# Two expert loops cut at 58 and 54 blocks with the rest in a branch, and a routing step moved ahead of an earlier branch

## The chip, the cores and the metric

The kernel runs on one core of a Trainium2 chip. The metric is device time in microseconds (us), the median of several runs. A core has five engines with instruction queues of their own: TensorE (PE) for matrix products, VectorE (DVE), ScalarE (ACT), GpSimd (POOL) and SyncE (SP). SP, ACT and POOL also issue DMA transfers. Engines wait for each other through semaphores. A branch in the program is taken by each engine for itself.

## What is computed

Two layers, each a graph network and then a mixture of experts, on x of 3125 nodes with 256 features and 50000 edges. Each of the four parts reads the layer-normalized x and is added to x. Only the mixtures matter here:

```python
# layer 0: 16 experts, the best 2 of a softmax, weighted
top_probs, top_idx = jax.lax.top_k(probs, 2)
dispatch = sum(one_hot(top_idx, 16) * (top_probs / sum(top_probs))[..., None], -2)
hidden = silu(x @ w1[e]) * (x @ w2[e])          # 512 wide, for each expert e
x = x + sum_e dispatch[:, e] * (hidden @ w3[e])
# layer 1: 8 experts, the best 2 of the scores, unweighted
h = gelu(x @ W1[e] + b1[e])                     # 512 wide
x = x + sum_e mask[:, e] * (h @ W2[e] + b2[e])
```

Every node picks two experts, so 6250 rows of work are shared out unevenly over the experts.

## The kernel before

The program runs in stages. Layer 0's graph part works on the transposed adjacency counts, in panels of 512 columns (convolution1, convolution2). While the last convolution's panels end, Router.panel finds for each node its two experts and its rank within each expert. A flag tells whether the edges came sorted; where they did not, a branch (L884 and L885) builds the graph in another way and repeats the layer. With these inputs the branch isn't taken, but each engine loads the flag, compares, and jumps over the code. At the place where it arrives it raises its own semaphore by the count of the code it left out; whoever comes after the branch waits for that arrival.

Behind the branch stand three steps. First, resident (L906): GpSimd issues 16 loads of 0.5 MB each, which bring w3 of all experts into SBUF (w3_all, 8.39 MB). Second, Router.route: rows of an expert are packed into blocks of 128 rows, no block mixes experts, and route works out for each block its expert (exp, expi) and its 128 node numbers (idx). It starts from the totals of each expert (L604, L607), forms each expert's first block (L622), compares block numbers with each node's block (L645, a vector operation of 64 x 25 elements a partition), multiplies by tile and row numbers (L649 on ScalarE, L650 on VectorE), and sums with 50 small matrix products (L652); three vector operations then make idx (L657 to L661). Third, experts.

How many blocks there are isn't known when the program is built. The kernel runs the largest number that can occur:

```python
def blocks_of(n_exp):
    return (2 * N + n_exp * (P - 1)) // P     # 64 for 16 experts, 56 for 8
```

Blocks beyond the last real one have a spare row as each of their nodes and cost the same work. In experts, a block does this: begin (SP loads the w1 and w2 of its expert, L934, into one of three buffers each; GpSimd gathers its 128 rows from DRAM with an indirect DMA, L940), hidden (TensorE transposes the rows, L401, and multiplies with the weights, L961: 8 products in layer 0, 4 in layer 1, where the weights all stay in SBUF), finish (TensorE transposes the hidden rows, L973, multiplies with w3, L980, VectorE makes y, L996 or L988, and GpSimd adds y to the rows in DRAM with an indirect DMA, L997). Blocks are begun two ahead, and finished two behind in layer 0, one behind in layer 1. GpSimd executes its queue in order: w3's 16 loads, then gathers and scatters as the blocks come. Its DMAs use eight completion semaphores in turn, so that a ninth waits for the first to land.

After layer 0's blocks, the next stage loads x from the same DRAM rows (xb0, L1045), and waits for all scatters. After layer 1's, one copy from DRAM to DRAM (L1215) brings the result out, which also waits for all scatters. The edges' flag decides a second branch, with an else, around layer 1's graph part (L1187).

Of the kernel before, what the change touches and what calls it, by code (L numbers as in the profile page):

```python
# [18 lines left out]
P = 128  # L19
# [33 lines left out]
def kernel(ctx: ExitStack, tc: tile.TileContext, a, out: bass.AP):  # L53
# [81 lines left out]
    def build_sorted(c):  # L135

        found = keep.tile([1, 1], F32, name="found")
        free = onehots[:, 3 * GW * (NF + P) :]  # L140
        sums = free[:, : 4 * NG].bitcast(F32)
        ohr = free[:, 4 * NG :][:, : P * WN].rearrange("p (w r) -> p w r", r=WN)
        gl = c.enter_context(tc.tile_pool(name="sl", bufs=1))
        gk = c.enter_context(tc.tile_pool(name="sk", bufs=2))

        def iota_of(pool, name, shape, pattern, base=0, mult=0, dtype=F32):
# [344 lines left out]
    def blocks_of(n_exp):  # L491
        return (2 * N + n_exp * (P - 1)) // P

    class Router:


# [2 lines left out]

        ohs_ = keep.tile([P, 2, NT, NE0], F16, name="ohs")  # L500
        high = keep.tile([P, 2, NT], F32, name="high")
        before_ = keep.tile([P, NT + 1, NE0], F16, name="before")

        def __init__(self, n_exp):
            self.n = n_exp
            self.ohs = self.ohs_[:, :, :, :n_exp]
            self.before = self.before_[:, :, :n_exp]
            self.rows = onehots.rearrange("p (c t r) -> p c t r", c=2, t=NT)

        def panel(self, small, c0, s, gates=None):  # L510
            n_exp, n, t0 = self.n, s.shape[1], c0 // P
# [80 lines left out]
                )  # L592

        def route(self, small):


            n_exp = self.n
            nb = blocks_of(n_exp)

            def tile_(name, shape, dtype=F32):  # L600
                return small.tile(shape, dtype, name=name)

            pc = ps_one("totals", [P, n_exp])
            nc.tensor.matmul(pc, ones16, self.before[:, NT, :], start=True, stop=True)  # L604

            cnt = tile_("cnt", [P, n_exp])
            nc.vector.tensor_scalar(cnt, pc, float(P - 1), None, op0=OP.add)  # L607
            cnti = tile_("cnti", [P, n_exp], I32)
            nc.vector.tensor_copy(cnti, cnt)
            nc.vector.tensor_single_scalar(cnti, cnti, 7, op=OP.arith_shift_right)  # L610
            nblk = tile_("nblk", [P, n_exp])
            nc.vector.tensor_copy(nblk, cnti)
            ends = [tile_(f"ends{i}", [P, n_exp]) for i in range(2)]
            nc.vector.tensor_copy(ends[0], nblk)
            d, cur = 1, 0
            while d < n_exp:
                nc.vector.tensor_add(ends[1 - cur][:, d:], ends[cur][:, d:], ends[cur][:, : n_exp - d])
                nc.vector.tensor_copy(ends[1 - cur][:, :d], ends[cur][:, :d])
                d, cur = 2 * d, 1 - cur
            ends = ends[cur]  # L620
            first = tile_("first", [P, n_exp], F16)
            nc.vector.tensor_sub(first, ends, nblk)  # L622

            past = tile_("past", [P, nb, n_exp])
            nc.vector.tensor_tensor(
                past, iota[:, :nb, None].to_broadcast([P, nb, n_exp]), ends[:, None, :].to_broadcast([P, nb, n_exp]),
                OP.is_ge,
            )
            exp = keep.tile([P, nb], F32, name=f"exp{n_exp}")
            nc.vector.tensor_reduce(exp, past, AX.X, OP.add)  # L630
            nc.vector.tensor_scalar(exp, exp, float(n_exp - 1), None, op0=OP.min)
            expi = keep.tile([1, nb], I32, name=f"expi{n_exp}")
            nc.vector.tensor_copy(expi, exp[:1])

            pi = ps_one("nodes", [P, 2, nb])
            for c in range(2):
                of = tile_("of", [P, NT, n_exp], F16)
                nc.vector.tensor_tensor(of, self.ohs[:, c], first[:, None, :].to_broadcast([P, NT, n_exp]), OP.mult)
                blk = tile_("blk", [P, NT])
                nc.vector.tensor_reduce(blk, of, AX.X, OP.add)  # L640
                blk16 = tile_(f"blk16_{c}", [P, NT], F16)
                nc.vector.tensor_add(blk16, blk, self.high[:, c, :])
                is_ = tile_(f"is_{c}", [P, nb, NT], F16)
                shape = [P, nb, NT]
                nc.vector.tensor_tensor(  # L645
                    is_, iota16[:, :nb, None].to_broadcast(shape), blk16[:, None, :].to_broadcast(shape), OP.is_equal
                )
                what = tile_(f"what{c}", [P, 2, nb, NT], F16)
                nc.scalar.activation(what[:, 1], is_, AF.Copy, scale=pcol)  # L649
                nc.vector.tensor_tensor(what[:, 0], is_, tiles16[:, None, :].to_broadcast(shape), OP.mult)  # L650
                for t in range(NT):
                    nc.tensor.matmul(  # L652
                        pi.rearrange("p a b -> p (a b)"), self.rows[:, c, t, :], what[:, :, :, t].rearrange("p a b -> p (a b)"),
                        start=(c == 0 and t == 0), stop=(c == 1 and t == NT - 1),
                    )
            none = tile_("none", [P, nb])
            nc.vector.tensor_scalar(none, pi[:, 0, :], 0.0, spare, op0=OP.is_equal, op1=OP.mult)  # L657
            node = tile_("node", [P, nb])
            nc.vector.scalar_tensor_tensor(node, pi[:, 0, :], float(P), none, op0=OP.mult, op1=OP.add)
            idx = keep.tile([P, nb], I32, name=f"idx{n_exp}")  # L660
            nc.vector.scalar_tensor_tensor(idx, node, -float(P), pi[:, 1, :], op0=OP.add, op1=OP.add)  # L661
            return idx, exp, expi


    class First:
# [147 lines left out]
    with ExitStack() as c:  # L813
# [62 lines left out]
        with ExitStack() as c1:  # L876
# [4 lines left out]
                nc.scalar.dma_start(t[NP:, :], behind[:, : t.shape[1]])  # L881
            f.weights2(c1)
            convolution2(f, False, c1.enter_context(tc.tile_pool(name="loads0", bufs=3)))
    sorted_ = nc.values_load(flag, min_val=0, max_val=1)  # L884
    with tc.If(sorted_ == 0):  # L885
        build_graph()
        degrees(0, NT)
        with ExitStack() as c:
# [7 lines left out]
            open_rows(c)  # L896
            f.weights2(c)
            convolution2(f, True, c.enter_context(tc.tile_pool(name="loads0", bufs=3)))


    def resident(pool, name, w):
# [4 lines left out]
            nc.gpsimd.dma_start(t[:, e], w[e].rearrange("(k p) n -> p k n", p=P))  # L906
        return t

    def experts(hids, wts, xnd, xb, n_exp, idx, expi, w_in, b_in, w_out, act, gated=None, b_out=None, stay=(), depth=1):

        n_in, n_hid = len(w_in), w_out.shape[1] // P
        stay = list(stay) + [None] * (n_in + 1 - len(stay))
        streamed = b_in is not None or None in stay
        wide = D if gated is None else D + 4

        sent, ran, regs = [], [], {}

# [32 lines left out]
            if any(t is not None for t in stay):  # L952
                regs[b] = expert_of(nc.tensor, ran, b)

        def hidden(b, weights, bi, xg):
            xT = hids.tile([P, KD, P], F32, name="xT")
            transpose_tile(xT, xg)
            ph = ps_wide("ph")
            for i in range(n_in):
                for k in range(KD):  # L960
                    ran.append(nc.tensor.matmul(  # L961
                        ph[:, i, :], xT[:, k, :], weight_of(b, weights, i, k), start=(k == 0), stop=(k == KD - 1)
                    ))
                    if i + k == 0 and b + 1 < nb:
                        register(b + 1)
            hid = hids.tile([P, n_hid * P], F32, name="hid", bufs=depth + 1)
            act(hid, ph, bi)
# [2 lines left out]
        def finish(b, hid, weights, xg):  # L970
# [13 lines left out]
                mine, bo = b_out  # L984
                nc.tensor.matmul(po, mine[:, b : b + 1].to_broadcast([mine.shape[0], P]), bo, start=False, stop=True)  # L985
            y = hids.tile([P, D], F32, name="y", bufs=2)
            if gated is None:
                nc.vector.tensor_copy(y, po)  # L988
            else:
                each = hids.tile([P, 2], F32, name="each")  # L990
                gate = hids.tile([P, 1], F32, name="gate")
                nc.vector.scalar_tensor_tensor(  # L992
                    each, xg[:, D + 2 :], gated[:, b : b + 1], xg[:, D : D + 2], op0=OP.is_equal, op1=OP.mult,
                    accum_out=gate,
                )
                nc.vector.tensor_scalar(y, po, gate, None, op0=OP.mult)  # L996
# [2 lines left out]
                in_=y, in_offset=None, compute_op=OP.add,  # L999
            )  # L1000

        nb = blocks_of(n_exp)
        register(0)
        ahead = [begin(0), begin(1)]
        open_ = []
        for b in range(nb):
            weights, bi, xg = ahead.pop(0)
            open_.append((b, hidden(b, weights, bi, xg), weights, xg))
            if len(open_) > depth:
                finish(*open_.pop(0))  # L1010
            if b + 2 < nb:
                ahead.append(begin(b + 2))
        for o in open_:
            finish(*o)

    ffn0 = ctx.enter_context(ExitStack())
    w3_all = resident(ffn0.enter_context(tc.tile_pool(name="res0", bufs=1)), "w3_all", a["L0_ffn_w3"])
    with ExitStack() as c:
        idx, exp, expi = router0.route(c.enter_context(tc.tile_pool(name="small0", bufs=1)))

    with ExitStack() as c:
        hids = c.enter_context(tc.tile_pool(name="hids0", bufs=2))
        wts = c.enter_context(tc.tile_pool(name="wts0", bufs=3))
# [1 line left out]
        def silu_gate(hid, ph, bi):  # L1025
# [1 line left out]
            nc.vector.tensor_mul(hid, hid, ph[:, 1, :])  # L1027

        experts(
            hids, wts, xnd0, xb0, NE0, idx, expi,  # L1030
            [a["L0_ffn_w1"], a["L0_ffn_w2"]], None, a["L0_ffn_w3"], silu_gate, gated=exp, stay=[None, None, w3_all], depth=2,
        )
    ffn0.close()

# [159 lines left out]


    with ExitStack() as c:
        idx, exp, expi = router1.route(c.enter_context(tc.tile_pool(name="small1", bufs=1)))
        mine = keep.tile([NE1, blocks_of(NE1)], F32, name="mine")
        nc.vector.tensor_scalar(mine, exp[:NE1], pcol[:NE1], None, op0=OP.is_equal)

    with ExitStack() as c:
        hids = c.enter_context(tc.tile_pool(name="hids1", bufs=2))
# [4 lines left out]
        def gelu(hid, ph, bi):  # L1207
# [1 line left out]
            nc.scalar.activation(hid, hid, AF.Gelu)  # L1209

        experts(
            hids, wts, xnd1, xb1, NE1, idx, expi, [a["L1_ffn_W1"]], a["L1_ffn_b1"], a["L1_ffn_W2"], gelu,
            None, (mine, b2e), [w1_all, w2_all],
        )
    nc.sync.dma_start(out, xb1[:N, :])  # L1215

# [30 lines left out]
```

## Time and profile before

| | |
|---|---|
| median of 3 runs | 1919.1 us (1915.95 to 1920.69) |
| the profiled execution, its span | 1919.9 us, 1918.1 us |
| busy: PE, DVE, ACT, POOL | 86%, 47%, 36%, 27% of the span |
| gathers and scatters of blocks | 120 each |
| blocks of layer 0 | about 671 to 1079 us |
| blocks of layer 1 | about 1596 to 1905 us |

A row of the timeline has the start in us from the span's start, the duration, the engine, the line, the operation, what it writes and reads, and how often; in brackets stands how long the engine was idle before it and what ended that. PE is busy nearly without a gap in both stretches of blocks. The stretch between 624 and 672 us, in which the choice of experts ends, is one of the idlest of the execution: PE is busy 16.2 of 48 us.

### The profile page before, as it was taken

The page shows a single profiled execution, that of the slowest core. Times are in us where ns is not written, and L with a number is a line of the kernel's source. Part 1 is how long each engine was busy: PE and PEld are TensorE (multiplying, and loading weights), DVE is VectorE, ACT ScalarE, POOL GpSimd, SP SyncE. Part 2 cuts the span into 40 slices and gives each one's busy share as a digit, 9 for nine tenths or more (in the row PEclk, how much of TensorE's full clock was granted, in tenths as well). Part 3 has the DMA queues.
Part 4 walks back from the last instruction along what each step waited for, and adds up shares of the span by engine and source line. Part 5 has one row for each costly group of instructions (what it writes and reads, how often), then busy time and mean ns, then how long its engine had stood idle before and what let it go on. Part 6 is the DMA issues. An engine that isn't in the chain of part 4 may idle for free. (4 is left out here: it accounts for less than half of the span.)

```text
span 1918.1 us, 24044 instructions
## 1 busy us (share of the span) xinstructions
PE 1652.2 (86%) x7618; PEld 1127.4 (59%) x7618; DVE 893.1 (47%) x2509; ACT 682.5 (36%) x1596; POOL 509.8 (27%) x543
## 2 busy tenths in 40 slices
PE   4899999799998399999999459789797647999995
PEld 3777777677777155665556336456565534556553
DVE  5866665246665423322233457456467452222221
ACT  2766666234442122222222246346363102222221
POOL 4411110100000334444443234014021202445442
PEclk9999999999998599999999769999998657999998
DMA  3311111611110687777777220000012603444444
GB/s 116 104 47 47 48 48 37 224 59 56 56 59 24 202 247 216 218 213 211 211 217 192 63 60 0 1 1 1 1 34 66 233 28 76 102 102 99 101 103 102
DMA packets 126765, 193.02 MB, mean 101 GB/s; under 512 B 15040, under 2 KB 71727, under 8 KB 126559
## 3 DMA queue, kind: packets, MB, share of 16 engines
q1 hardware_dynamic: 93036, 137.34, 22.6%
q0 software_dynamic: 28544, 50.74, 12.7%
q10 hardware_dynamic: 5042, 3.23, 0.6%
q8 instruction: 67, 1.10, 0.2%
q14 instruction: 76, 0.61, 0.1%
HBM read 148.74 MB, written 45.72 MB: 101 GB/s over the span
## 5 line engine op out<-in xcount | busy, mean ns | idle before, releaser
L723 PE MATMUL pa<-blk,hl 128*128 128x512 f32 (+1 forms) x1400 | 366.9, 401 | 1.3 <-ACT blk L434 1.3
L997 POOL DMA_INDIRECT xb<-y,idx x120 | 190.9, 1591 | 326.7 <-DVE each L992 221.2
L723 PEld LDWEIGHTS pa<-blk,hl 128*128 128x128 f32 x1400 | 249.3, 196 | 43.7 <-ACT blk L434 1.8
L434 ACT CAST blk<-at 128x512 fp32r<-128x512 fp8e4 (+1 forms) x378 | 208.3, 572 | 137.2 <-PE pa L723 59.4
L961 PE MATMUL ph<-w,xT 128*128 128x512 f32 x512 | 238.8, 610 | 5.6 <-ACT xT L402 0.8
L980 PE MATMUL pe<-w_all,hTs 128*128 x960 | 227.2, 379 | 3.0 <-ACT hTs L976 3.0
L980 PEld LDWEIGHTS pe<-w_all,hTs 128*128 128x128 f32 x960 | 182.1, 190 | 78.1 <-issue 55.5
L436 DVE CAST blk<-at 128x512 fp32r<-128x512 fp8e4 (+1 forms) x392 | 167.8, 438 | 93.2 <-PE pa L723 56.4
L1136 PE MATMUL pc<-blk,g 128*128 128x512 f32 (+1 forms) x525 | 150.2, 420 | 23.9 <-ACT blk L434 13.7
L940 POOL DMA_INDIRECT xg<-xnd,idx x120 | 117.9, 982 | 168.4 <-DVE idx L661 86.0
L961 PEld LDWEIGHTS ph<-w,xT 128*128 128x128 f32 x512 | 92.6, 191 | 114.4 <-issue 88.3
L402 ACT COPY xT<-pt 128x256 f32<-128x256 f32 x195 | 72.6, 372 | 227.8 <-PE pt L401 226.0
L1027 DVE TENSOR_TENSOR hid<-hid,ph 128x512 f32<-128x512 f32 x64 | 44.0, 688 | 232.8 <-ACT hid L1026 232.8
L438 POOL CAST blk<-at 128x512 fp32r<-128x512 fp8e4 (+1 forms) x105 | 66.1, 629 | 292.2 <-PE pc L1136 290.3
L1136 PEld LDWEIGHTS pc<-blk,g 128*128 128x128 f32 x525 | 92.7, 201 | 66.2 <-DVE blk L436 22.3
L1026 ACT ACTIVATE hid<-ph 128x512 f32<-128x512 f32 x64 | 38.2, 597 | 219.4 <-PE ph L961 219.4
L961 PE MATMUL ph<-w_all,xT 128*128 x224 | 112.0, 624 | 4.2
L271 ACT ACTIVATE at<-pcount 128x400 fp8e4<-128x400 f32 x196 | 97.4, 502 | 49.4 <-PE pcount L267 48.2
L267 PE MATMUL pcount<-onehots 128*128 128x100 f16 x784 | 93.8, 270 | 3.0 <-ACT at L271 1.5
L267 PEld LDWEIGHTS <-onehots 128*128 128x128 f16 x784 | 68.8, 118 | 28.3 <-issue 12.8
L906 POOL DMA_DIRECT2D w_all<-in_L_ffn_w_dram x16 | 12.1, 767 | 268.2 <-PE totals L604 263.6
L1209 ACT ACTIVATE hid<-hid 128x512 f32<-128x512 f32 x56 | 35.3, 630 | 133.8 <-DVE hid L1208 133.8
(250 smaller groups left out, 2284.2 us busy)
## 6 DMA issues: line engine op xcount, KB each, us to landing
w<-in_L_ffn_w_dram SPq DMA_DIRECT2D x128, 512.0 KB, 4.7
bin<-in_L_ffn_b_dram SPq DMA_DIRECT2D x56, 256.0 KB, 3.5
w_all<-in_L_ffn_w_dram POOLq DMA_DIRECT2D x16, 512.0 KB, 10.7
w_all<-in_L_ffn_W_dram POOLq DMA_DIRECT2D x16, 512.0 KB, 10.8
h1d<-hl SPq DMA_DIRECT2D x25, 256.0 KB, 2.0
hl<-h1d SPq DMA_DIRECT2D x25, 256.0 KB, 5.3
xp<-in_x_dram SPq DMA_DIRECT2D x12, 512.0 KB, 4.7
mine<-own SPq DMA_DIRECT2D x12, 512.0 KB, 3.9
```

The lines of the kernel that those rows point to most:

```text
L267: nc.tensor.matmul(pw[:, w * NF : (w + 1) * NF], ohl[:, b, :, w], ohk[:, b, :, w], start=True, stop=True)
L271: nc.scalar.activation(at8[o // PW][:, :, o % PW : o % PW + 4 * WN].rearrange("p k (w r) -> p w k r", r=WN), pw[:, : 4 * NF].rearrange("p ...
L402: nc.scalar.copy(dst, pt)
L434: nc.scalar.copy(dst, src)
L436: nc.vector.tensor_copy(dst, src)
L438: nc.gpsimd.tensor_copy(dst, src)
L723: nc.tensor.matmul(pa[:, m, :w], parts[k][:, i, m * P : (m + 1) * P].bitcast(one), blk, start=(k == 0 and i == 0), stop=(k == NT - 1 and i ...
L940: nc.gpsimd.indirect_dma_start(out=xg, out_offset=None, in_=xnd[:, :], in_offset=bass.IndirectOffsetOnAxis(ap=idx[:, b : b + 1], axis=0),)
L961: ran.append(nc.tensor.matmul(ph[:, i, :], xT[:, k, :], weight_of(b, weights, i, k), start=(k == 0), stop=(k == KD - 1)))
L980: nc.tensor.matmul(po, hT[:, j, :], weight_of(b, weights, n_in, j), start=(j == 0), stop=(j == n_hid - 1 and b_out is None))
L997: nc.gpsimd.indirect_dma_start(out=xb[:, :], out_offset=bass.IndirectOffsetOnAxis(ap=idx[:, b : b + 1], axis=0), in_=y, in_offset=None, co ...
L1136: nc.tensor.matmul(pc[:, :w], g[:, k].rearrange("p i q -> p (i q)").bitcast(one), blk, start=(k == 0), stop=False,)
```

## The change

Four edits. (1) usual(n_exp) gives 58 blocks for 16 experts and 54 for 8. experts runs so many; the further blocks, up to 64 and 56, stand in a branch that is taken when route found more blocks than that (the cell more). (2) The call of route for layer 0 moves up, behind the last convolution and ahead of the flag's branch; it is repeated inside that branch, where the layer is repeated. What route returned are now fields of the router. (3) In route, the comparison reads a table of block numbers that GpSimd writes (blocks, the iota), where it read one row of numbers stretched over the tiles. (4) The cell found moves to another pool of tiles.

```diff
+    def usual(n_exp):
+        return -(-(2 * N + n_exp * P // 2) // P) + 1
...
         def route(self, small):
...
-            nc.vector.tensor_copy(expi, exp[:1])
+            nc.vector.tensor_copy(self.expi, exp[:1])
+            nc.vector.tensor_scalar(self.more, ends[:1, n_exp - 1 :], float(usual(n_exp)), None, op0=OP.is_gt)
+            blocks = tile_("blocks", [P, nb, NT], F16)
+            nc.gpsimd.iota(
+                blocks, pattern=[[1, nb], [0, NT]], base=0, channel_multiplier=0, allow_small_or_imprecise_dtypes=True
+            )
...
-                nc.vector.tensor_tensor(
-                    is_, iota16[:, :nb, None].to_broadcast(shape), blk16[:, None, :].to_broadcast(shape), OP.is_equal
-                )
+                nc.vector.tensor_tensor(is_, blocks, blk16[:, None, :].to_broadcast(shape), OP.is_equal)
...
             convolution2(f, False, c1.enter_context(tc.tile_pool(name="loads0", bufs=3)))
+    with ExitStack() as c:
+        router0.route(c.enter_context(tc.tile_pool(name="small0", bufs=1)))
     sorted_ = nc.values_load(flag, min_val=0, max_val=1)
     with tc.If(sorted_ == 0):
         build_graph()
...
+        with ExitStack() as c:
+            router0.route(c.enter_context(tc.tile_pool(name="small0", bufs=1)))
...
-        nb = blocks_of(n_exp)
-        register(0)
-        ahead = [begin(0), begin(1)]
-        open_ = []
-        for b in range(nb):
...
+        def run(b0, until):
+            sent.clear()
+            ran.clear()
+            register(b0)
+            ahead = [begin(b) for b in range(b0, min(b0 + 2, until))]
+            open_ = []
+            for b in range(b0, until):
+                weights, bi, xg = ahead.pop(0)
+                open_.append((b, hidden(b, weights, bi, xg, until), weights, xg))
+                if len(open_) > depth:
+                    finish(*open_.pop(0))
+                if b + 2 < until:
+                    ahead.append(begin(b + 2))
+            for o in open_:
+                finish(*o)
+
+        run(0, usual(n_exp))
+        more = nc.values_load(router.more, min_val=0, max_val=1)
+        with tc.If(more == 1):
+            run(usual(n_exp), blocks_of(n_exp))
...
     w3_all = resident(ffn0.enter_context(tc.tile_pool(name="res0", bufs=1)), "w3_all", a["L0_ffn_w3"])
     with ExitStack() as c:
-        idx, exp, expi = router0.route(c.enter_context(tc.tile_pool(name="small0", bufs=1)))
-
-    with ExitStack() as c:
```

## The prediction

> **What bounds the kernel now.** I read the time itself first. The profiled execution took 1919.9 us, its span is 1918.1, so 1.8 lie around it; the median of the runs is 1919.1 (1915.95 to 1920.69). The sum below is made against the profiled execution and then carried to the median, 0.8 lower. Of the runs' spread, 0.3% (5.8 us) is about what a measurement can tell from no change.
>
> Then the two loops over expert blocks, in the timeline and in the chain that ended last (columns: start, duration, engine and work).
>
> ```profile
> 1041.73 3.70 PE L961 MATMUL ph<-w,xT 128*128 128x512 f32 x8
> 1047.89 3.70 PE L961 MATMUL ph<-w,xT 128*128 128x512 f32 x8
> ...
> 1880.41 1.98 PE ph L961 x4
> 1885.63 1.98 PE ph L961 x4
> ```
>
> TensorE sets the pace of both: a block of layer 0 costs 6.16 us (1047.89 - 1041.73), one of layer 1 costs 5.22, and the last blocks cost what the others do. Layer 0 runs 64 blocks, layer 1 runs 56.
>
> Third, the timeline where the choice of layer 0 ends and its blocks begin.
>
> ```profile
> 637.62 0.16 DVE L587 TENSOR_SCALAR high<-high 128x2 f32<-128x2 f32 x1
> 642.05 0.17 DVE L607 TENSOR_SCALAR cnt<-totals 128x16 f32<-128x16 f32 x1 [4.27 <-PE totals L604]
> 642.19 6.81 POOL L906 DMA_DIRECT2D w_all<-in_L_ffn_w_dram  x9 [263.61 <-PE totals L604]
> 648.29 1.81 DVE L645 TENSOR_TENSOR is<-iota,blk 128x1600 f16<-128x1600 f16 x1
> 650.50 1.00 DVE L650 TENSOR_TENSOR what<-is,tiles 128x1600 f16<-128x1600 f16 x1
> 658.13 0.75 POOL L906 DMA_DIRECT2D w_all<-in_L_ffn_w_dram  x1 [0.76 <-DMA w_all<-in_L_ffn_w_dram]
> 663.96 0.22 DVE L661 SCALAR_TENSOR_TENSOR idx<-node,nodes 128x64 int32<-128x64 f32 x1
> 665.07 1.04 POOL L940 DMA_INDIRECT xg<-xnd,idx  x1 [6.19 <-DVE idx L661]
> 671.14 0.66 PE L401 MATMUL pt<-ident,xg 128*128 128x128 f32 x2 [7.80 <-DMA xg<-xnd,idx]
> ```
>
> VectorE crosses the branch between L587 and L607. At once GpSimd starts the 16 loads of w3 (0.5 MB each), and they run under the 22 us of route; when idx is ready GpSimd is free to gather, and TensorE starts at 671.14.
>
> Fourth, the branch and the DMA rate in the same stretch (first fence: duration, then start; second: the last columns are granted clock, DMA share, GB/s).
>
> ```profile
> L885 DVEq COMPARE_BRANCH  x1: 72/72/72, 638.2 to 638.2; - x1
> L885 PEldq COMPARE_BRANCH  x1: 3422/3422/3422, 636.2 to 636.2; - x1
> L885 DVEq EVENT_SEMAPHORE  x1: 21/21/21, 641.4 to 641.4; - x1
> L885 POOLq INC_SWDGE_SEM  x1: 616/616/616, 388.2 to 388.2; - x1
> ```
>
> ```profile
> 656.00:660.00 4.00, 4.00 (x19) 2.25 (x18) 0.00 (x0) 0.00 (x0) 1.50 (x2) 0.50 1.02 346
> 668.00:672.00 4.00, 0.66 (x2) 0.29 (x2) 0.23 (x2) 0.11 (x1) 2.54 (x3) 0.50 1.03 363
> 672.00:676.00 4.00, 3.28 (x6) 1.65 (x7) 0.23 (x2) 1.91 (x3) 1.89 (x2) 0.50 1.05 378
> ```
>
> A jump is not free: 3.8 us pass on VectorE from its last instruction (637.62) to its first step behind the jump (641.4). And the 16 DMA engines are full, near 350 GB/s, from 644 on.
>
> **The blocks left out.** The reference's routing, evaluated for its inputs, fills 58 blocks in layer 0 and 53 in layer 1. The test is "more than 58" and "more than 54", so neither branch is taken. No expert's count stands closer than 18 below a multiple of 128, so rounding doesn't tip it. 6 x 6.16 = -37.0 us; 2 x 5.22 = -10.4 us. The drain of the last blocks is the same at either number.
>
> **The route moved ahead of the branch.** Three effects.
> (1) Its small operations now queue on VectorE between those of the last panel's ranks, without the crossing. Before, the interval from L587 to L607 is 4.4 us; two interleaved chains of 0.2 us steps also fill each other's gaps, about another 0.8. First is thus ready near 639.4 rather than 644.6: 5.2 earlier.
> (2) The comparison L645 reads a full table from GpSimd rather than a broadcast row. It then has the form of L650, 1.00 instead of 1.81 us. Only its first half is on the path (the second runs under TensorE's first 25 matmuls): -0.8 in layer 0, and likewise -0.7 in layer 1. Between no gain and this, I take this. The table itself costs 3.4 us on GpSimd (the IOTAs of 400 and 512 elements take 0.97 and 1.19 us), in layer 0 under the last panel, where GpSimd stands idle since 388, in layer 1 near 1568, 13 us before it is read. Uncovered, it would cost 3.4. The extra comparison that makes "more" is one 0.17 us step.
> (3) The w3 loads now stand behind the whole route. They are issued in the code after the branch, their first one waits for VectorE's arrival there, and VectorE arrives only after idx: 663.96 - 5.2 - 0.8 = 658.0, plus the 3.8 of the crossing = 661.8. GpSimd's first w3 load follows 0.8 later (641.42 to 642.19 before) at 662.6. SP's w1 and w2 loads wait for the same arrival. GpSimd's order is w3 sixteen times, then the gathers; so what is queued behind the wait is everything that TensorE needs.
>
> How long the loads take: the engines reached full rate 2.3 us after the first issue before, so from 664.9 here. Ahead of the first gather stand w3, 8.39 MB, and six half-megabyte loads from SP (three buffers of two), 3.15 MB, together 11.5 MB. At 352 GB/s that is 32.8 us: all landed at 697.7, the gather and its 0.13 MB at 698.1. TensorE starts 27.0 us later than at 671.14.
>
> [...] The trace's row: a w3 load lands after 4.6 us at least and 10.7 in the median with eight in flight, which suits a queue served in order. Without that order, a gather could pass as soon as it is issued, which needs load 9 landed (GpSimd reuses eight completion slots): near 687.5, plus the 6.1 that a gather takes (665.07 to 671.14): 693.6, or +22.5. I take +27.0 and keep +18 (SP's loads given the smaller share) to +31 (a rate of 315 GB/s).
>
> **The two new branches.** Each engine loads "more" and jumps over the extra blocks. For all but GpSimd that lies under the landing of the last scatter. The next reader of xb waits for GpSimd's INC_SWDGE_SEM, which stands behind the scatter's landing and behind the jump. Layer 1: GpSimd's sequencer reaches its closing drain at 1900.6; 0.5 for the load, 3.7 for the jump (384.1 to 387.8 in the first branch), some 0.3 of waits and 0.62 for the increment give 1905.8, against 1904.62 for the copy before: +1.2. The same at layer 0's end, +1.2. Bounds: 0.6 (the increment alone) to 5.3 each (all of it behind the landing).
> [...] The row above has 3422 ns on TensorE and a gap of 3.1 on VectorE between branch and next step. [...]
>
> **Sum.** +27.0 (later start) - 37.0 + 1.2 - 0.7 - 10.4 + 1.2 = -18.7 us. 1919.9 becomes 1901.2 for a profiled execution, and the median 1900.4; I say 1900.5. With the bounds of the start and of the ends, the likeliest case spans 1890 to 1908.
>
> **Rivals.**
> *The late w3 loads are hidden anyway.* GpSimd gathers first, or w3 isn't needed until the first second-stage product 16 us later (L980 at 687.55). Then the start moves by -2.2 (6.0 earlier idx, 3.8 for the crossing) and the time is about 1871. Against it: GpSimd's program order, and DMA engines already full at 1.0.
> *The crossings cost more.* At 5.3 us each, [...] 8 us come on top: 1909. For it: TensorE's later branch takes 5.1 us instead of 3.4. Against it: TensorE has slack there.
> *Slower.* The two queues together at the stage's start carry much less than one alone. Place: 665 to 698. It decides from a delay of 45.7 us, that is below 224 GB/s; slower by over 0.3% needs 51.5, below 201. At 175 GB/s, half the measured rate, the time is 1933. Against it: 363 and 378 GB/s with both queues at work at 668 to 676.
> *The change doesn't do what it says.* Were there a 59th block, all 64 would run, with a second fill and drain of some 17 us (the 16.4 from first transpose to first L980 before, and a little more): about 1955. The counts speak against it.
>
> **How the numbers follow.** Likeliest case 0.78; w3 hidden 0.06; dearer crossings 0.09; slower by the loads 0.04; branch taken 0.01; 0.02 for what I don't see. Eight in ten lie within 1890 to 1909, the likeliest case and most of the dearer crossings; both tails stay out. Faster by over 0.3%: 0.91 (the first three cases but for a little of the third). Within 0.3%: 0.04. Slower: 0.05.
>
> **What would show it.** Counts of 112 for the gathers and scatters; 464 matmuls of the first stage (8 a block) in layer 0 instead of 512, and 216 (4 a block) instead of 224 in layer 1; the w3 loads beginning near 662.6 with the gathers only after them; TensorE's first transpose near 698 with its wait on the gather; DMA share 1.0 from 665 to 698; L645's successor near 1.0 us; the load of x and the final copy about 1 us later after their last scatter. It is wrong if the transposes start before 690 or after 705, if the comparison keeps its 1.8, or if the branch code of the extra blocks shows instructions.

## The result

The median went from 1917.95 us (four runs on this chip, 1915.95 to 1920.69) to 1904.98 us (1903.21 to 1908.91): a ratio of 0.9932, 95% interval 0.9915 to 0.9949, or 13.0 us less. The forecast was 1900.5, 18.7 us less. Direction and range held; 5.7 us of the gain are missing. The profiled execution of the changed kernel is its slowest, 1908.91 us (span 1907.0), so what follows goes by marks inside the trace, not by that total.

### The profile page after: what moved, and what is told of

Same layout as the page of the kernel before. It is cut to its first block, busy times and chain, and to the rows that moved or that the text cites. A ratio compares the mean times of both kernels' runs of the same rounds, so it can differ in the third digit from the quotient of the medians.

```text
span 1907.0 us, 23502 instructions
## 1 busy us (share of the span) xinstructions
PE 1608.3 (84%) x7446; PEld 1100.1 (58%) x7446; DVE 878.0 (46%) x2475; ACT 672.1 (35%) x1572; POOL 495.0 (26%) x529
## 5 line engine op out<-in xcount | busy, mean ns | idle before, releaser
L731 PE MATMUL pa<-blk,hl 128*128 128x512 f32 (+1 forms) x1400 | 366.8, 401 | 5.2 <-ACT blk L434 5.2
L731 PEld LDWEIGHTS pa<-blk,hl 128*128 128x128 f32 x1400 | 249.1, 196 | 47.6 <-ACT blk L434 5.8
L1010 POOL DMA_INDIRECT xb<-y,idx x112 | 178.3, 1592 | 286.7 <-DVE each L1005 200.2
L974 PE MATMUL ph<-w,xT 128*128 128x512 f32 x464 | 216.4, 610 | 5.1 <-ACT xT L402 0.8
L993 PE MATMUL pe<-w_all,hTs 128*128 x896 | 212.1, 379 | 2.7 <-ACT hTs L989 2.7
L993 PEld LDWEIGHTS pe<-w_all,hTs 128*128 128x128 f32 x896 | 169.9, 190 | 72.7 <-issue 51.7
L1153 PE MATMUL pc<-blk,g 128*128 128x512 f32 (+1 forms) x525 | 150.4, 420 | 23.2 <-ACT blk L434 12.5
L953 POOL DMA_INDIRECT xg<-xnd,idx x112 | 110.3, 985 | 130.5 <-PE pt L401 50.8
L974 PEld LDWEIGHTS ph<-w,xT 128*128 128x128 f32 x464 | 83.9, 191 | 104.0 <-issue 80.2
L1044 DVE TENSOR_TENSOR hid<-hid,ph 128x512 f32<-128x512 f32 x58 | 39.9, 688 | 210.7 <-ACT hid L1043 210.7
L401 PE MATMUL pt<-ident,xg 128*128 128x128 f32 x224 | 46.7, 292 | 49.7 <-DMA xg<-xnd,idx 49.7
L643 POOL IOTA blocks<- 128x1600 f16 (+1 forms) x2 | 4.7, 2332 | 296.3 <-PE pa L731 245.1
```

Of the source, the lines that this page charges most:

```text
L401: nc.tensor.transpose(pt[:, k, :], src[:, k * P : (k + 1) * P], ident)
L731: nc.tensor.matmul(pa[:, m, :w], parts[k][:, i, m * P : (m + 1) * P].bitcast(one), blk, start=(k == 0 and i == 0), stop=(k == NT - 1 and i ...
L953: nc.gpsimd.indirect_dma_start(out=xg, out_offset=None, in_=xnd[:, :], in_offset=bass.IndirectOffsetOnAxis(ap=idx[:, b : b + 1], axis=0),)
L974: ran.append(nc.tensor.matmul(ph[:, i, :], xT[:, k, :], weight_of(b, weights, i, k), start=(k == 0), stop=(k == KD - 1)))
L993: nc.tensor.matmul(po, hT[:, j, :], weight_of(b, weights, n_in, j), start=(j == 0), stop=(j == n_hid - 1 and b_out is None))
L1010: nc.gpsimd.indirect_dma_start(out=xb[:, :], out_offset=bass.IndirectOffsetOnAxis(ap=idx[:, b : b + 1], axis=0), in_=y, in_offset=None, co ...
```

## The profile after

The two loops, in the timeline (columns as before: start, duration, engine and work). The period is as it was, 6.17 and 5.22 us, only with fewer blocks.

```profile
1041.54 3.70 PE L974 MATMUL ph<-w,xT 128*128 128x512 f32 x8
1047.71 3.70 PE L974 MATMUL ph<-w,xT 128*128 128x512 f32 x8
...
1868.53 1.98 PE L974 MATMUL ph<-w_all,xT 128*128 x4
1873.75 1.98 PE L974 MATMUL ph<-w_all,xT 128*128 x4
```

The page's costliest groups have the counts: 464 matmuls of the first stage in layer 0 (58 blocks of 8), 112 gathers and 112 scatters (58 + 54).

```profile
L1010 POOL DMA_INDIRECT xb<-y,idx x112 | 178.3, 1592 | 286.7 <-DVE each L1005 200.2
L974 PE MATMUL ph<-w,xT 128*128 128x512 f32 x464 | 216.4, 610 | 5.1 <-ACT xT L402 0.8
...
L953 POOL DMA_INDIRECT xg<-xnd,idx x112 | 110.3, 985 | 130.5 <-PE pt L401 50.8
```

The stretch where the choice of layer 0 ends, in the timeline of the changed kernel:

```profile
641.98 0.17 DVE L616 TENSOR_SCALAR cnt<-totals 128x16 f32<-128x16 f32 x1
643.56 0.16 DVE L598 TENSOR_SCALAR high<-high 128x2 f32<-128x2 f32 x1
648.45 1.01 DVE L657 TENSOR_TENSOR is<-blocks,blk 128x1600 f16<-128x1600 f16 x1
663.13 0.22 DVE L670 SCALAR_TENSOR_TENSOR idx<-node,nodes 128x64 int32<-128x64 f32 x1
667.44 6.83 POOL L918 DMA_DIRECT2D w_all<-in_L_ffn_w_dram  x9 [41.40 <-DVEq L895]
688.76 0.75 POOL L918 DMA_DIRECT2D w_all<-in_L_ffn_w_dram  x1 [1.27 <-DMA w_all<-in_L_ffn_w_dram]
691.11 1.04 POOL L953 DMA_INDIRECT xg<-xnd,idx  x1 [1.60 <-DMA w_all<-in_L_ffn_w_dram]
703.32 1.30 PE L401 MATMUL pt<-ident,xg 128*128 128x128 f32 x5 [40.80 <-DMA xg<-xnd,idx]
...
718.18 1.89 PE L993 MATMUL pe<-w_all,hTs 128*128 x8
```

The last row is the first product of the second stage, the one with w3. Before, it was this one:

```profile
687.55 1.89 PE L980 MATMUL pe<-w_all,hTs 128*128 x8
```

The first load of w3 stood between L607 and the comparison before, 22 us ahead of idx. Here it stands 4.3 us behind idx, its wait ends with VectorE's arrival behind the branch, and the first gather stands behind the last w3 load. The branch (duration in ns, then start) and the DMA rates of the same stretch (last three columns: the granted clock, which is the share of its full speed that TensorE was given, the busy share of the DMA engines, and GB/s):

```profile
L895 PEldq COMPARE_BRANCH  x1: 3652/3652/3652, 658.9 to 658.9; - x1
L895 DVEq COMPARE_BRANCH  x1: 72/72/72, 663.8 to 663.8; - x1
L895 DVEq EVENT_SEMAPHORE  x1: 21/21/21, 666.6 to 666.6; - x1
```

```profile
656.00:660.00 4.00, 4.00 (x20) 2.24 (x18) 0.00 (x0) 0.00 (x0) 0.00 (x0) 0.50 0.02 4
...
672.00:676.00 4.00, 0.00 (x0) 0.00 (x0) 0.00 (x0) 0.00 (x0) 2.86 (x5) 0.50 1.04 369
...
696.00:700.00 4.00, 0.00 (x0) 0.00 (x0) 0.00 (x0) 0.00 (x0) 2.12 (x3) 0.50 1.03 348
```

The DMA engines are nearly empty under the route (4 GB/s, where the same stretch had 346 before) and full afterwards (348 to 369 GB/s from 672 to 700), with TensorE standing still (no product in any of these windows).

Laid side by side, the two traces tell where the time went. "Again" is a second profiled execution of the changed kernel from the experiments below; all numbers are shifts against the trace of before, in us.

| mark | changed | again |
|---|---|---|
| ScalarE's copy of the last `xp` before the second convolution (L764, now L772) | -0.2 | 0.0 |
| first product of the second convolution (L723, L731) | +3.8 | +3.9 |
| last step of the ranks (L587, L598) | +5.9 | +5.7 |
| first transpose of layer 0's blocks | +32.2 | +32.5 |
| first second-stage product (L980, L993) | +30.6 | +30.5 |
| last scatter of layer 0 | -6.4 | -6.4 |
| first load of x behind it (L1045, L1062) | -4.6 | -4.5 |
| first second-stage product of layer 1 | -1.9 | -8.0 |
| final copy | -11.1 | -16.8 |

Two of these shifts were in no step of the prediction: +3.8 at the first product and another +2.0 before the ranks end. Below the load of x the two executions of one program differ by up to 6 us, so no smaller difference is read there. Some of it is seen at the start of layer 1's blocks, where in the slower one the second gather landed later (the second pair of transposes stands 2.30 us behind the first, 0.93 in the other) and the first eight products took 6.47 us against 5.21 (10.96 us from the first transpose to the first second-stage product, 8.32 in the other, 8.04 before).

## Experiments

The four intervals that the experiments are read by come from each profiled execution's timeline: A from ScalarE's copy of `xp` to the last step of the ranks; B from there to TensorE's first transpose of a block; C from the same step to the first second-stage product; D from that product to the last scatter of layer 0.

| kernel | time, us | ratio to before (95%) | A | B | C | D |
|---|---|---|---|---|---|---|
| before (medians of the four comparisons) | 1915.85 to 1917.95 | 1 | 256.98 | 33.5 | 49.9 | 387.8 |
| changed | 1904.98 | 0.9932 (0.9915 to 0.9949) | 263.08 | 59.8 | 74.6 | 350.8 |
| changed, again | 1902.58 | 0.9927 (0.9907 to 0.9946) | 262.68 | 60.4 | 74.8 | 350.9 |
| the cut alone | 1871.88 | 0.9777 (0.9755 to 0.9799) | 254.61 | 33.8 | 49.6 | 351.0 |
| the move alone | 1943.80 | 1.0140 (1.0118 to 1.0162) | 256.95 | 61.2 | 75.0 | 387.7 |
| `found` kept | 1901.10 | 0.9928 (0.9908 to 0.9949) | 259.22 | 60.4 | 75.0 | 350.9 |
| no table | 1903.59 | 0.9933 (0.9914 to 0.9953) | 261.05 | 61.3 | 76.5 | 351.0 |
| `found` kept, no table | 1898.97 | 0.9905 (0.9886 to 0.9923) | 257.16 | 61.2 | 76.5 | 351.0 |
| the cut without its branches | 1869.34 | 0.9750 (0.9732 to 0.9768) | 256.64 | 36.1 | 51.4 | 350.8 |
| gathers first | 1900.18 | 0.9918 (0.9901 to 0.9935) | 263.11 | 28.8 | 69.4 | 353.4 |
| gathers first, w3 behind SP's first loads | 1894.38 | 0.9886 (0.9867 to 0.9906) | 263.11 | 29.4 | 63.9 | 352.6 |

Four executions with both `found` moved and the table give A between 262.68 and 263.11. A of the cut alone is 2.4 below that of before with the same work in it (TensorE's granted clock from 380 to 420 was 0.95 there and 0.90 before), so one difference of 2 us in one execution says little; the ones used below recur.

### The two halves apart

The cut alone: `usual`, `run` and the new branches as changed; the route of layer 0 back behind the branch, the old comparison, `found` kept.

```diff
-    with ExitStack() as c:
-        router0.route(c.enter_context(tc.tile_pool(name="small0", bufs=1)))
     sorted_ = nc.values_load(flag, min_val=0, max_val=1)
...
     w3_all = resident(ffn0.enter_context(tc.tile_pool(name="res0", bufs=1)), "w3_all", a["L0_ffn_w3"])
+    with ExitStack() as c:
+        router0.route(c.enter_context(tc.tile_pool(name="small0", bufs=1)))
```

> Only the first part of the change: 58 and 54 blocks and a branch for more, with the end of the choice of layer 0 behind the branch for unsorted edges as before, no table, `found` kept. Theory: the blocks left out are worth 6 x 6.16 + 2 x 5.22 = 47.4 us, the crossings of the two new branches cost 1.9 and 1.2 us (from the trace of the changed kernel), so 44.3 us below the kernel before: about 1873.7, first transpose of the blocks near 671 as before. Rival: the crossings or a longer program cost several us more: 1877 to 1880.

The move alone: the changed kernel with `found` kept, no table, and

```diff
-        run(0, usual(n_exp))
-        more = nc.values_load(router.more, min_val=0, max_val=1)
-        with tc.If(more == 1):
-            run(usual(n_exp), blocks_of(n_exp))
+        run(0, blocks_of(n_exp))
```

> Only the second part: the end of the choice of layer 0 ahead of the branch for unsorted edges, with all 64 and 56 blocks, no new branch, no table, `found` kept. Theory: the loads of w3, and the gathers behind them, start only after the choice, so the first transpose stands some 26 to 27 us later than 671.1 and the first second-stage product some 25 later; the time rises by about 25.5 us, to 1943.4. Rival: the late start in the changed kernel comes from the other parts (the table, the new addresses): less than 10 us, below 1928.

Measured: 44.9 us less for the cut (1916.78 to 1871.88; 42.7 by the ratio), 27.0 us more for the move (26.8 by the ratio). D fell by 36.8 with the cut and not with the move; B and C rose by 27.7 and 25.1 with the move and not with the cut. The timeline of the cut alone shows w3 loading ahead of the comparison and the gather free when idx is ready:

```profile
638.58 6.80 POOL L911 DMA_DIRECT2D w_all<-in_L_ffn_w_dram  x9 [261.14 <-PE totals L613]
644.77 1.81 DVE L653 TENSOR_TENSOR is<-iota,blk 128x1600 f16<-128x1600 f16 x1
660.45 0.22 DVE L668 SCALAR_TENSOR_TENSOR idx<-node,nodes 128x64 int32<-128x64 f32 x1
661.56 1.04 POOL L946 DMA_INDIRECT xg<-xnd,idx  x1 [5.93 <-DVE idx L668]
667.90 0.66 PE L401 MATMUL pt<-ident,xg 128*128 128x128 f32 x2 [8.07 <-DMA xg<-xnd,idx]
```

Both theories held. The second rival fell. Of the first only the low end, 1877, is still inside the interval of the ratio, and the trace of the cut speaks against it: behind the last scatters it has 2.0 us more than before in layer 0 and 0.1 in layer 1. The move costs more than half of what the cut brings, and the cut alone is the fastest kernel of the study that also covers inputs with more blocks: 0.9777 of before.

### The two late losses

In the changed kernel `found`, one number, went from the pool that lives through the kernel to a pool (`sl`) that is given back before the second convolution. In the built program the convolution's first `blk` buffer then covers its address. There ScalarE's first cast waits for VectorE's step `flag <- top1, found` (done at 383.13; the cast starts at 385.14) and stands behind ScalarE's four DMA issues; before, two casts stood ahead of them. The timelines, before and then changed:

```profile
379.35 0.62 ACT L434 CAST blk<-at 128x512 fp32r<-128x512 fp8e4 x1 [0.87 <-issue]
382.02 8.36 PE L723 MATMUL pa<-blk,hl 128*128 128x512 f32 x23 [0.96 <-ACT blk L434]
383.09 0.83 ACTq L881 DMA_DIRECT2D xnd<-rows  x2
383.33 0.14 DVE L858 TENSOR_TENSOR flag<-top,found 1x1 int32<-1x1 f32 x1
```

```profile
382.95 0.82 ACTq L889 DMA_DIRECT2D xnd<-rows  x2
382.98 0.15 DVE L866 TENSOR_TENSOR flag<-top,found 1x1 int32<-1x1 f32 x1
385.14 1.14 ACT L434 CAST blk<-at 128x512 fp32r<-128x512 fp8e4 x2 [4.28 <-DMA xnd<-rows]
385.81 4.63 PE L731 MATMUL pa<-blk,hl 128*128 128x512 f32 x10 [4.90 <-ACT blk L434]
```

To try it, `found` goes back; its slot comes from sharing a tile between `more` and the flag.

```diff
-        found = gl.tile([1, 1], F32, name="found")
+        found = keep.tile([1, 1], F32, name="found")
-        mores = keep.tile([1, 2], I32, name="more")
+        mores = keep.tile([1, 3], I32, name="more")
-    flag = keep.tile([1, 1], I32, name="flag")
+    flag = Router.mores[:, 2:]
```

> The changed kernel with the one-element tile `found` back in the pool that lives through the kernel (the slot for it comes from putting `more` and the flag in one tile). Theory: in the changed kernel the first `blk` buffer of the second convolution has the address of `found`, so ScalarE's first cast waits for the step that reads `found`, and is queued behind ScalarE's DMA issues; that is the 3.8 us by which TensorE's first product there moved (382.02 to 385.81). Then this kernel's first product is near 382.0 again, and the time is 3.8 us below the changed kernel's 1905.0: about 1901.2, or 16.8 under the kernel before. Rival: the 3.8 us come from elsewhere (the order of the DMAs, the clock of TensorE there): first product still near 385.8, time 1905.

The first product came 1.42 us behind the copy of `xp`, as before (1.38), against 5.33 in the changed kernel; A fell by 3.86. This part of the theory is shown. By the ratio the time is the changed kernel's within the noise (0.9928 against 0.9932), so the saving shows in the trace and not in this comparison of times.

The second loss is the table. The IOTA, the instruction that writes it, runs on GpSimd for 2.49 us in the tail of the last panel, and until it ended two of VectorE's casts stood (2.48 and 2.22 us), and a copy queued between them (2.40). The changed kernel's timeline (the steps took 0.17, 0.28 and 0.17 us in the trace of before; the last line was `0.52 <-DVE agg`):

```profile
623.55 2.49 POOL L643 IOTA blocks<- 128x1600 f16 x1 [245.12 <-PE pa L731]
623.59 2.48 DVE L592 CAST low<-low 128x8 f16<-128x8 int32 x1
623.67 2.40 DVE L737 COPY agg<-pa 128x128 f32<-128x128 f32 x1
623.87 2.22 DVE L593 CAST high<-ranki 128x8 f32<-128x8 int32 x1
...
626.15 1.22 PE L413 MATMUL pl<-w_L_gnn_W_l,agg 128*128 128x256 f32 x2 [2.67 <-DVE agg L737]
```

Taken away, with the broadcast comparison back:

```diff
-            blocks = tile_("blocks", [P, nb, NT], F16)
-            nc.gpsimd.iota(
-                blocks, pattern=[[1, nb], [0, NT]], base=0, channel_multiplier=0, allow_small_or_imprecise_dtypes=True
-            )
...
-                nc.vector.tensor_tensor(is_, blocks, blk16[:, None, :].to_broadcast(shape), OP.is_equal)
+                nc.vector.tensor_tensor(
+                    is_, iota16[:, :nb, None].to_broadcast(shape), blk16[:, None, :].to_broadcast(shape), OP.is_equal
+                )
```

> The changed kernel without the table: the broadcast comparison of the kernel before, in both layers, and no IOTA. Theory: the IOTA on GpSimd (2.49 us at 623.55) holds up VectorE's copy of the last aggregate and with it TensorE by 2.1 us in layer 0 and 0.3 in layer 1, while the table saves 0.8 and 0.7 us in the comparisons. So without it the choice of layer 0 ends its last ranks 2.1 us earlier, the comparisons take 1.8 and 1.6 us again, and the time moves by -2.1 + 0.8 - 0.3 + 0.7 = -0.9 us: about 1904, not to be told from the changed kernel by the time alone; the interval from the first product of the second convolution to the last step of the ranks tells it (257.75 us in the changed kernel, 255.60 before). Rival: VectorE's stand at 623.6 has another cause: that interval stays at 257.7, and the time rises by 1.5 us to 1906.5.

A fell by 2.03. In the same place and order, without the IOTA:

```profile
623.49 0.17 DVE L592 CAST low<-low 128x8 f16<-128x8 int32 x1
623.57 0.28 DVE L735 COPY agg<-pa 128x128 f32<-128x128 f32 x1
623.91 2.07 PE L413 MATMUL pl<-w_L_gnn_W_l,agg 128*128 128x256 f32 x4 [0.53 <-DVE agg L735]
```

So the IOTA is what held VectorE there. B is 59.8 to 60.4 us in the three executions with the move and the table and 61.3 here, about the 0.8 of the comparison more, and the time did not move (0.9933). C rose by more (74.6 to 76.5), but this can't be put down to the table: the move alone has no table either, and its C is 75.0. In all three kernels without the table but with the move, B is 61.2 or 61.3; what differs is the stretch from the first transpose to the first second-stage product, 13.8 to 15.3 us, and why is open.

The changed kernel again, and both repairs together, timed side by side:

> The changed kernel itself once more, so that the others can be compared with it on the same chip: 1905, within 3 us.

> The changed kernel with `found` kept and without the table: both late losses undone. Theory: from ScalarE's copy of the last xp before the second convolution to the last step of the ranks 256.9 us, as before the change (changed kernel 263.1, with `found` kept alone 259.2, without the table alone 261.1), the comparisons 1.8 and 1.6 again; the time 3.8 + 0.9 = 4.7 us below the changed kernel on the same chip, about 1900.3. Rival: the two losses don't add up in the time, because what follows (the loads of w3) absorbs them: within 1.5 us of the changed kernel.

A is 257.16 with both repairs, 5.5 below the changed kernel beside it, and within 0.2 of before. The time is 1898.97 against 1902.58: 3.6 us less (4.2 by the ratios) where 4.7 were expected. The two intervals of the ratio still overlap by 0.0016, so the sign rests on A together with the time, and the times alone don't exclude the rival, a difference within 1.5 us. With both losses gone the kernel stands 16.9 us below before (18.2 by the ratio), which is also about the sum of the two halves (-44.9 + 27.0 = -17.9).

### What the new branches cost

The cut alone, with the branch and the code behind it left out:

```diff
         run(0, usual(n_exp))
-        more = nc.values_load(router.more, min_val=0, max_val=1)
-        with tc.If(more == 1):
-            run(usual(n_exp), blocks_of(n_exp))
```

> The cut alone (58 and 54 blocks, the choice of layer 0 behind its branch as before) without the two new branches and the code behind them; inputs that need more blocks would be left out, so this measures only what the branches cost. Theory: the scatter of the last block of each layer is followed by the next reader of its rows as in the kernel before (3.8 us in both layers, from the issue of the last scatter to the next transfer), where the kernels with the branch have 5.7 in layer 0; with what the last blocks themselves lose, 3.1 us in all, so about 47.4 below the kernel before, 1869, and 3 below the cut with branches. Rival: the branches cost nothing that the next transfer doesn't wait for anyway: no difference.

1869.34 against 1871.88, not timed side by side; the intervals of the ratios overlap. The traces give the place. From the last scatter of layer 0 to the first load of x: 3.9 us before and here, 5.7 in the changed kernel, 5.8 in the cut. From the last scatter of layer 1 to the final copy: 3.8 before, 3.8 in the changed kernel, 3.9 in the cut, 3.7 here. The rows of the new branch on GpSimd's queue in the changed kernel (executed at the end of each layer: shortest, median and longest duration in ns, then the first and the last start) say why:

```profile
L1033 POOLq COMPARE_BRANCH  x2: 53/56/58, 1069.1 to 1889.9; - x2
L1033 POOLq INC_SWDGE_SEM  x2: 812/1078/1343, 1072.6 to 1890.2; - x2
```

At the end of layer 0, 3.5 us pass between branch and increment, which runs from 1072.6 to 1073.9 where the last scatter landed at 1072.63; at the end of layer 1 only 0.3, and the increment is done at 1891.0, before that scatter landed (1893.40). So the branches cost 1.8 to 2.0 us in layer 0 and at most 0.2 in layer 1. (B of this kernel is 2.3 us longer than that of the cut, in the one execution profiled; why is open.) No run here shows why the jump in layer 1 was the quicker one.

### What holds the start of the blocks

The prediction said that everything TensorE needs stands behind the sixteen w3 loads on GpSimd's queue. So the changed kernel with three gathers ahead of them; `later` holds the function that issues the sixteen loads, which `resident` no longer issues itself for w3:

```diff
                 if b + 2 < until:
                     ahead.append(begin(b + 2))
+                if b == 0:
+                    for load in later:
+                        load()
```

> The changed kernel with one change of order on GpSimd's queue: the gathers of the first three blocks are issued ahead of the sixteen loads of w3 instead of behind them. Theory: the gathers stand in the queue behind w3, and that alone holds TensorE's first transpose until 703.3; with them first, TensorE starts near 674 and works on three blocks' first stage while w3 lands; then w3 is the limit, and the first second-stage product starts when it has landed, near 704 instead of 718.2. The time falls by about 14 us, to 1890.5. Rival: TensorE's start is held by the loads of w1 and w2 on SP's queue, which share the full DMA engines with w3, so the order on GpSimd's queue is worth little: first second-stage product later than 714, time above 1901.

B fell from 60.4 to 28.8 us, so the gathers' place does set TensorE's first transpose. But C fell only from 74.8 to 69.4, not by 14, and the time by 2.4 us (1902.58 to 1900.18). TensorE works through the first stage of three blocks and stands again. The expectation failed. So did its rival in its numbers (the product came at 711.83, and the transposes do start early), but the loads on SP's queue that it named are part of what follows. The timeline and the windows:

```profile
671.15 0.66 PE L401 MATMUL pt<-ident,xg 128*128 128x128 f32 x2 [9.79 <-DMA w<-in_L_ffn_w_dram]
694.16 0.75 POOL L920 DMA_DIRECT2D w_all<-in_L_ffn_w_dram  x1 [1.44 <-DMA w_all<-in_L_ffn_w_dram]
711.83 3.75 PE L1000 MATMUL pe<-w_all,hTs 128*128 x8 [20.22 <-DMA xg<-xnd,idx]
```

```profile
668.00:672.00 4.00, 0.66 (x2) 0.29 (x2) 0.23 (x2) 0.03 (x1) 3.69 (x5) 0.50 0.91 267
672.00:676.00 4.00, 1.57 (x5) 0.95 (x6) 0.23 (x2) 1.67 (x3) 3.97 (x6) 0.50 1.05 384
...
704.00:708.00 4.00, 0.00 (x0) 0.00 (x0) 0.00 (x0) 0.00 (x0) 0.50 (x1) 0.50 1.04 362
708.00:712.00 4.00, 0.17 (x1) 0.20 (x2) 0.00 (x0) 0.00 (x0) 0.00 (x0) 0.50 0.98 343
```

The product's row names a gather, but the wait was for w3: by the landing times in the trace its last load, issued at 694.16, landed at 711.69, 0.14 us ahead of the product, and the first gather behind it only at 712.3. The DMA engines are full to the end (343 GB/s from 708 to 712). All eleven windows from 668 to 712 add up to 15.5 MB. That is w3 (8.39), seven gathers (0.93) and twelve half-megabyte loads from SP (6.29), 15.6 in all, where I had counted six such loads: TensorE, by working early, freed the buffers of three blocks, and SP's loads for the next three took their share while w3 was still on its way. The bytes agree with it: without those six loads, 3.15 MB, it would be 12.5. The changed kernel shows the two queues sharing as well: by its trace SP's first six loads landed one by one from 673.1 to 694.8, among w3's sixteen, which landed from 671.8 to 702.5.

To try that, w3 goes onto SP's own queue, between its loads for the third block and those for the fourth:

```diff
-                nc.gpsimd.dma_start(t[:, e], w[e].rearrange("(k p) n -> p k n", p=P))
+                (nc.gpsimd if later is None else nc.sync).dma_start(t[:, e], w[e].rearrange("(k p) n -> p k n", p=P))
```

> The kernel with the gathers first, with the sixteen loads of w3 issued by SP's queue between its loads for the first three blocks and those for the fourth, instead of by GpSimd. Theory: with the gathers first, the first second-stage product came only 69.4 us after the last step of the ranks (74.8 in the changed kernel) because SP's loads for blocks 3 to 5, whose buffers TensorE freed early, shared the DMA engines with w3: 8.4 + 12 x 0.52 + 0.9 = 15.6 MB moved in that time, as the DMA rates show. With w3 ahead of those loads, 11.5 MB are ahead of the product: at 0.36 MB per us that is 32 us from about 668.5 on the same clock, so the product comes about 8 us earlier, 61.4 us after the last step of the ranks, and the time falls by 8 us from 1900.2 to about 1892. Rival: what SP's loads for blocks 3 to 5 took was spare (w3's own loads, eight at a time, were the limit), so nothing is gained: 69 us again and about 1900.

```profile
703.21 3.75 PE L1000 MATMUL pe<-w_all,hTs 128*128 x8 [17.87 <-DMA w<-in_L_ffn_w_dram]
```

C fell to 63.9, 5.5 of the 8 us expected, and the time to 1894.38 (5.8 us less, 6.1 by the ratios). The rival fell: the share that SP's later loads took was not spare. The rest is mostly, by an estimate that no run tried, an item that I left out of the 11.5 MB: the gathers, 0.93 MB, at 0.355 MB per us 2.6 us. Here too the last load of w3 landed just ahead of the product, at 702.86. So the limit on the first second-stage product was, in both orders, the number of bytes ahead of w3's last one, at the rate of full DMA engines (343 to 384 GB/s from 672 to 712 with the gathers first, 348 to 395 from 668 to 704 here). In each order tried, w3 and the first blocks' loads cost an estimated 32 us (11.5 MB at that rate) when they start only after the route. This kernel is still 22.5 us behind the cut alone (20.9 by the ratios), where w3 loads under the route; some 4 us of that are the two late losses, which it still has.

## Why the prediction came out as it did

*The blocks left out* (-37.0 and -10.4): right. D fell by 387.8 - 350.8 = 37.0. In layer 1 the stretch from the first to the last second-stage product went from 285.8 to 275.6, by 10.2.

*Effect 1, the route interleaved and without the crossing* (-5.2), *and effect 2, the comparison* (-0.8): right. From the last step of the ranks to idx it was 26.34 and is 19.57 us: 6.8 less, where 6.0 were forecast. Without the table it is 20.37, so 0.8 of it is the comparison.

*Effect 3, w3 behind the route*: right in mechanism and size. Shifted by the 5.9 us by which the ranks ended late, the forecast of 698.1 for the first transpose becomes 704.0; it came at 703.32. The crossing took 3.5 us (663.1 to 666.6; 3.8 forecast), the rate was 348 to 369 GB/s (352). The move alone confirms it: +27.7 for the transpose. The gathers did land in order behind w3: in the profiled execution of the changed kernel the last w3 load landed at 702.54 and the first gather at 702.91, in "again" at 702.87 and 703.25. What was incomplete is the reason that the prediction put in front, the gathers' place in the queue. Two limits lie one behind the other here: the gathers, and w3 itself. With the gathers freed, w3 landed at 711.69 and held the product, and only 2.4 us came back. The rival "w3 hidden anyway" would not have come true with the gathers first either, and its price of 1871 for that case was too low by far (1900.18; by an estimate 1896, if the two losses below are worth the 3.6 to 4.2 us that undoing them brought). The fill behind the first transpose was 1.6 us shorter than before (14.9 against 16.4), which the sum held fixed.

*The two crossings* (+1.2 each): mis-sized both ways. Layer 0 cost about 1.9, layer 1 at most 0.2; the sum, 2.4 forecast and about 2.1 found, is right by luck. The step that failed is the jump of 3.7 us assumed at both ends, and with it the increment's place behind the scatter's landing: in layer 1 it began 0.5 us after that scatter was issued. From branch to increment it took 0.3 us at that end and 3.5 at the other.

*The table* (3.4 us, costed at nothing because GpSimd stands idle): this step failed. I asked whether GpSimd was free and not who would stand while it works. The IOTA took 2.49 us, on the path by way of VectorE: +2.0.

*`found`*: absent from the prediction. The diff moves one tile of one element between pools, and I took it for bookkeeping. It cost +3.9.

Together the two make 5.9 us in the trace, and 5.7 us of the gain are missing. That the numbers meet so closely is luck. At the last scatter of layer 0 the forecast was 27.0 - 37.0 = -10.0, and the trace has -6.4, 3.6 short: the shorter route (0.8) and the shorter fill (1.6) had given back the rest. Undoing both losses brought 3.6 us as well (4.2 by the ratios). The last 2 us of the 5.7 lie behind that scatter, where two executions of one program differ by up to 6, and no run settles them. The kernel with both losses undone has neither term; for it the steps of the prediction, without the 0.8 and 0.7 of the comparisons, add up to -17.2, and it measured -16.9 (by the ratio -18.2). So the sum describes that kernel to within the 2 us or so that the times can't resolve.

## What to carry to other kernels

When a step is moved, ask first what was running beneath it: the 22 us of route had hidden 8.4 MB of loads, and with the cover taken away the kernel was 27 us slower, the 6 us that the route gained already counted. Price every line of a diff, also one that only moves a tiny tile: a tile's pool decides which later buffer takes its address, and with it who waits for whom (`found` cost 3.9 us in the trace). Behind the limit that is removed, look for the next one in the same bytes: here the gathers in front of the full DMA queue brought the first transpose 31.6 us forward and the first second-stage product only 5.4; fewer bytes ahead of w3's last one brought that product another 5.5, and with the earlier start of the cut alone it came 49.6 us after the ranks' last step where the changed kernel has 74.6.

## What the hardware showed unexpectedly

An IOTA on GpSimd, which reads no tile (its row has none behind the arrow), held VectorE's casts for its whole 2.49 us, and with them a copy queued behind the first, but not every VectorE instruction. In layer 1 of the changed kernel the statistics, the aggregation and the reciprocal pass beneath it at their usual length (0.43, 0.18 and 0.16 us; before the change 0.39 to 0.43, 0.15 to 0.18 and 0.15 to 0.18), and only the scaling of rows stands (0.70 us for 0.41); it ends 0.15 us after the IOTA, which ends at 1566.37:

```profile
1564.20 2.17 POOL L643 IOTA blocks<- 128x1400 f16 x1 [51.22 <-PE po L413]
1564.62 0.43 DVE L387 BATCH_NORM_STATS2 st<-x 128x6 f32<-128x256 f32 x1
1565.62 0.16 DVE L391 RECIPROCAL rstd<-rstd 128x1 f32<-128x1 f32 x1 [0.36 <-ACT rstd L390]
1565.82 0.70 DVE L393 TENSOR_SCALAR rows<-x,mv,rstd 128x256 f32<-128x256 f32 x1
```

Why some of VectorE's instructions stood and others passed is not in the trace, and no run here tests it.

From GpSimd's compare-and-branch, itself 53 to 58 ns, to the increment behind it 0.3 us passed at one end and 3.5 at the other, in the same program. And TensorE, which with the gathers first had stood for 20.2 us, came back at half clock: its granted clock was 0.50 from 712 to 716 us and 0.75 from there to 720, and its first eight second-stage products took 3.75 us where eight take 1.89 in the steady loop. In the changed kernel the slow time fell into the fill: the clock was 0.50 from the first transpose (703.32) to 707 and back at 1.00 from 709 on, ahead of that product (718.18). This fits that of the 5.4 us saved in C only 2.9 were left at the last scatter.
